# Two layers of gated cross-attention and experts: layer 0's step in another order, the experts' scores in another PSUM bank

## The chip, the cores and the metric

One core of a Trainium2 chip. The metric is the device time of one execution in microseconds; the median of three runs before is 2903.76 us (2900.48 to 2905.07). In the profile PE is TensorE's matmuls, PEld its weight loads, DVE VectorE, ACT ScalarE, POOL GpSimd and SP the engine that issues most DMAs. "L599" is line 599 of the kernel before.

## The reference

The input x is 64 sequences of 128 positions by 128 features; a context has 64 sequences of 77 positions. Two layers follow one another, each of a cross-attention and an expert block, added to x through a gate:

```python
x = x + tanh(g_xattn[0]) * L0_xattn(ctx, ctx, layernorm(x), ...)   # 16 heads, features exp(z), exp(-z)
x = x + tanh(g_ffn[0])   * L0_ffn(layernorm(x), ...)               # 8 experts, silu(g) * u, inner 336
x = x + tanh(g_xattn[1]) * L1_xattn(layernorm(x), ctx, ctx, ...)   # 16 heads, relative positions
x = x + tanh(g_ffn[1])   * L1_ffn(layernorm(x), ...)               # 8 experts, top 2, relu(h)**2
```

Layer 0's attention maps queries, keys and values of each head to 16 features, takes softmax(q k / sqrt(128)), weighs the value features and multiplies the 256 outputs by fc_w. Its expert block has a router (softmax over 8 experts) and a small "actor" network that chooses how many of the experts count for a position. Every expert is computed for every position; a position's score for an expert, or 0, multiplies that expert's output row:

```python
for e in range(E):
    g = einsum('bsh,ih->bsi', hidden, gate_w[e])
    u = einsum('bsh,ih->bsi', hidden, up_w[e])
    y = einsum('bsi,hi->bsh', silu(g) * u, down_w[e])
    out = out + scores[..., e:e + 1] * y
```

## The kernel before

**Units and groups.** Layer 0's attention works on units of two sequences (32 units), its expert block and the whole of layer 1 on groups of four sequences (16 groups). Two units make a group.

**Layer 0's step.** Step k is a software pipeline over five pieces of work, each a Python generator whose parts are cut by `yield`:

- `l0_features(k)`, five parts: loads x and context (xg, cg), layer norm, transposes into pt and copies (L295 to L299); the projection pz (L302) and four Exp; transposes pv of the value features with copies to va (L318, L320); the split of the features into three bf16 parts (`split3`, L126 to L129: two casts on DVE, two subtractions on POOL); then ten DMAs through DRAM that stack them as qst and kst (dq, dk, then L331 and L333).
- `l0_maxima(k-1)`, seven parts: six banks of scores S (L346) with a maximum each (L349); then the transposition pn (L354), whose three bf16 parts n go by three DMAs into rows 96 to 98 of qst (L362).
- `l0_weighted(k-2)`, nine parts: the scores ST again (L387), now with the maximum folded in, Exp to P (L390), and the weighted sum AV (L376); then through DRAM to the normalized o (`normalize`, L437).
- `l0_project(k-3)`, one part: the output product pf (L411) and the sum x1 (L413).
- in even steps from 4 on `route`, six parts, for the group whose second half `l0_project` has just made: layer norm; transposes ptf (L449); router and actor product pr; logits pl (L469 to L474); softmax and ranks on DVE; and `scores_out`, whose transposes pp (L590) give the scores s3 in bf16 (L593).

Beside them runs the "tape", the expert blocks: 33 parts per group in layer 0 (`l0_ffn`), 24 in layer 1 (`l1_ffn`), some 16 of them in each step of layer 0. A part is one block of hidden units (gate product pg, up product pu, three matmuls each, then tanh and multiplications to t, and its two halves hh and hl) or one expert's output: `score_in` spreads the expert's score over all partitions by a matmul with a selection matrix (pb, `spread`, L599) and a copy to sb (L604), six matmuls make the output rows py, and `add_expert` multiplies py by sb (ys, L613; L610 for the first expert) and adds to acc. Once per group of layer 0 another `spread` makes the scale sl (L548) for the leftover hidden units, whose output rows are collected in one py over five blocks. `flush` (L570 on) transposes acc into po and stores a finished group.

**The order.** `weave` runs the parts of all pieces in order of due times. A row `(lo, hi, pri)` of `PLAN` spreads a piece's parts evenly from lo to hi, in shares of the step; parts due at the same time go in the order of the list, in which `out` stands first. With `pri` above 0 the part's instructions are emitted under `high_priority(offset=pri)`. From the emitted program the tile framework makes a fixed order of instructions on each engine, sets the waits, and gives buffers out; at run time every engine's queue is worked off in that order.

**The banks.** PSUM has eight banks of 128 x 512 float32. In layer 0 they are: `pmisc` (tag misc), `pS`, `pST`, `avp`, `pY` (tag y), and three `pGU` (tag gu). The pools misc, S, ST and y have one buffer each, so that a tile there waits until the tile before it has been read. Users of misc in layer 0 are pt, pz, pv (twice), pn, pf, pl, pp and pb; users of y are py and po. The units of layer 1 use misc for pc, px, pz (three), pv, po1, po2 and pf, its routing for ptf, pr, pl and pp, and its experts for pb.

**Other buffers that matter here.** xg has four buffers, kst and va three, qst three, o two, hh, hl and t three each, sb one, x1 three.

After layer 0's 34 steps a transition joins the last unit's output product and the last routing of layer 0 to the first units of layer 1, in a step of its own that takes its numbers from `PLAN["out"]` and `PLAN["rt0"]`.

Of the kernel before, what the change touches and what calls it, by code (L numbers as in the profile page):

```python
# [10 lines left out]
F32 = mybir.dt.float32  # L11
# [30 lines left out]
def weave(tc, streams):  # L42
# [18 lines left out]
PARTS0, PARTS1 = 33, 24  # L61

PLAN = dict(
    out=(0, 0.2, 2000),
    wei=(0, 0.7, 0),
    max=(0.2, 0.95, 1000),
    fea=(0.2, 0.6, 1000),
    out1=(0.25, 0.4, 600),
    att1=(0.1, 0.95, 0),
    rel1=(0.37, 0.93, 0),  # L70
# [7 lines left out]
    prjT=(0, 0.55, 1000),  # L78
    attL=(0.1, 0.4, 500),
    prjL=(0.2, 0.3, 500),  # L80
    rt0=(0.1, 1, 500),
    rt1=(0.45, 0.7, 1000),
)

# [11 lines left out]
class Net:  # L96
# [498 lines left out]

    def spread(self, w, s3):

        pb = self.pmisc.tile([128, 512], F32, tag="misc", name="pb")
        self.nc.tensor.matmul(pb, lhsT=w, rhs=s3, start=True, stop=True)  # L599
        return pb  # L600

# [442 lines left out]
    def run(self, ngroups):  # L1044
# [25 lines left out]
        nun = ngroups * 2  # L1070
        st = {}
        for k in range(nun + 2):
# [13 lines left out]
            if k == 1:  # L1086
                with tc.issue_after(self.last_dma.ins):
# [11 lines left out]
        self.banks = itertools.cycle(((self.pS, "S"), (self.pST, "ST")))  # L1099
        s1 = {}  # L1100
        h0, h1 = (0, 0, 2), (0, 2, 2)
        self.step([(self.l0_project(nun - 1, st.pop(nun - 1), self.xs), 1, *PLAN["out"]),
                   (self.route(ngroups - 1), 6, *PLAN["rt0"]),
                   (self.l1_project(*h0, s1), 8, *PLAN["prjT"]),
                   (self.l1_relate(h0, s1), 7, *PLAN["relT"])], 27, PLAN["t0"])
        self.step([(self.l1_attend(s1[h0], 2), 13, *PLAN["attL"]),
# [140 lines left out]
```

## Time and profile before

| | us |
|---|---|
| median of three runs | 2903.76 (2900.48 to 2905.07) |
| the profiled execution | 2871.89 |
| its span, first to last instruction | 2870.2 |
| mean granted TensorE clock in it | 0.921 |
| spread matmul pb (L599), 265 records | 409 ns each, 108.3 in all |
| copy sb (L604), 256 | 587 ns each, 150.3 in all |
| multiplication ys (L613), 224 | 684 ns each, 153.2 in all |
| output product pf (L411), 256 matmuls of 128 columns | 312 ns each, 40.9 in all |
| layer 0's steps | about 0 to 1400 us; in the steady part a pair of steps takes about 87 us |
| the transition | about 1400 to 1600 us |
| layer 1 | about 1500 to 2870 us |

The profiled execution is shorter than the runs' median by 1.1%. The busy time of an engine is the time in which one of its instructions ran; a wait is idle time of an engine, put down to what released it last. Of the time in which an engine waits, only that which the end of the program depends on costs anything.

### The profile page before, as it was taken

How to read it: one execution, taken by the hardware profiler on the slowest of the kernel's cores; microseconds unless marked ns; L12 is line 12 of the kernel's file. 1: busy time of each engine (PE TensorE's matmuls, PEld its weight loads, DVE VectorE, ACT ScalarE, POOL GpSimd, SP SyncE). 2: the span in 40 equal slices, each digit the busy share in tenths (PEclk: the TensorE clock that was granted, in tenths of full speed). 3: DMA queues.
4: the chain of work that ended last, by engine and by line, in shares of the span. 5: the costliest groups of instructions: out<-in, count | busy, mean ns of one | idle time of the engine just before them, and what ended most of it. 6: DMA issues, size and time to landing. Idle time of an engine off the chain costs nothing.

```text
span 2870.2 us, 61032 instructions
## 1 busy us (share of the span) xinstructions
PE 2452.1 (85%) x23631; PEld 1668.7 (58%) x23638; DVE 1935.3 (67%) x4054; ACT 1579.2 (55%) x3030; POOL 1574.0 (55%) x1508
## 2 busy tenths in 40 slices
PE   3788898888888888988887878898988889889887
PEld 2455665666566565656554556566665666556654
DVE  3468787777878778777764555566566666656655
ACT  2455565555555555555543445566655556556556
POOL 4455555565545555455645535565555556555556
PEclk9989999999999999999986778899999999999998
DMA  6743534544445445343244655554554556555500
GB/s 144 163 103 96 106 91 83 116 98 95 97 84 105 107 93 101 87 85 77 77 84 108 137 104 119 116 110 108 109 115 104 118 119 126 116 105 113 108 16 8
DMA packets 504412, 290.56 MB, mean 101 GB/s; under 512 B 264614, under 2 KB 480814, under 8 KB 504027
## 3 DMA queue, kind: packets, MB, share of 16 engines
q1 hardware_dynamic: 476475, 246.28, 42.8%
q10 hardware_dynamic: 27648, 40.38, 4.0%
q8 instruction: 186, 3.05, 0.4%
q14 instruction: 103, 0.84, 0.1%
HBM read 147.19 MB, written 138.60 MB: 100 GB/s over the span
## 4 chain that ended last, share of the span: by engine, by line
PE 42%; DVE 19%; DMA 18%; POOL 8%; issue 7%; ACT 4%; SPq 3%; ACTq 0%; POOLq 0%; DVEq 0%
PE py L156 3%; PE ST L827 3%; PE py L157 3%; DMA qst<-dq 2%; DMA qst<-n 2%; PE py L158 2%; PE AV L376 2%; PE pz L156 2%; DVE t L508 2%; PE pg L156 2%; POOL hl L987 2%; PE S L770 2%; DVE t L509 2%; DMA kst<-dk 2%; PE ST L387 2%
## 5 line engine op out<-in xcount | busy, mean ns | idle before, releaser
L515 POOL TENSOR_TENSOR hl<-t,hh 128x512 fp32r<-128x512 f32 x336 | 454.0, 1357 | 345.3 <-ACT hh L514 339.0
L987 POOL TENSOR_TENSOR hl<-t,hh 128x512 fp32r<-128x512 f32 x256 | 345.2, 1362 | 111.6 <-ACT hh L986 111.1
L819 POOL TENSOR_TENSOR sc<-sc,mx 128x308 f32<-128x308 f32 x256 | 192.1, 752 | 216.0 <-DVE mx L818 139.5
L507 ACT ACTIVATE t<-pg 128x512 f32<-128x512 f32 x336 | 200.7, 598 | 160.6 <-PE pg L158 104.3
L514 ACT CAST hh<-t 128x512 fp32r<-128x512 f32 x336 | 207.8, 619 | 137.4 <-DVE t L509 58.0
L613 DVE TENSOR_TENSOR ys<-sb,py 128x512 f32<-128x512 f32 x224 | 153.2, 684 | 190.0 <-ACT sb L604 105.0
L828 ACT ACTIVATE rel<-ST 77x512 f32<-77x512 f32 x256 | 157.9, 617 | 187.3 <-PE ST L827 185.7
L508 DVE SCALAR_TENSOR_TENSOR t<-t,pg 128x512 f32<-128x512 f32 x336 | 226.8, 675 | 40.7 <-ACT t L507 40.2
L509 DVE TENSOR_TENSOR t<-t,pu 128x512 f32<-128x512 f32 x336 | 226.7, 675 | 10.8 <-PE pu L158 3.8
L604 ACT COPY sb<-pb 128x512 f32<-128x512 f32 x256 | 150.3, 587 | 134.7 <-PE pb L599 88.5
L817 DVE TENSOR_TENSOR sc<-S,rq 128x308 f32<-128x308 f32 x256 | 121.4, 475 | 147.8 <-PE ST L827 73.2
L986 ACT CAST hh<-t 128x512 fp32r<-128x512 f32 x256 | 158.5, 624 | 109.8 <-PE py L158 82.7
L614 POOL TENSOR_TENSOR acc<-acc,ys 128x512 f32<-128x512 f32 x96 | 133.6, 1391 | 154.5 <-DVE ys L613 154.2
L390 ACT ACTIVATE P<-ST 77x512 f32<-77x512 f32 x256 | 151.1, 591 | 120.3 <-PE ST L387 115.5
L979 ACT ACTIVATE t<-pz 128x512 f32<-128x512 f32 x256 | 153.3, 599 | 71.6 <-POOL hl L987 64.3
L827 PE MATMUL ST<-ident,sc 128*128 128x128 f32 (+1 forms) x1024 | 182.8, 307 | 5.1 <-ACT sg L776 1.6
L349 DVE TENSOR_REDUCE mx<-S 128x5 f32<-128x385 f32 (+1 forms) x192 | 110.3, 576 | 107.4 <-PE S L346 106.5
L156 PE MATMUL pu<-xh,wu_h 128*128 128x512 f32 x336 | 159.1, 473 | 21.9 <-DVE t L508 20.7
L156 PE MATMUL pg<-xh,wg_h 128*128 128x512 f32 x336 | 161.4, 480 | 15.7 <-DVE t L509 10.2
L157 PE MATMUL py<-hl,wd_h 128*128 128x512 f32 x336 | 150.9, 449 | 23.3 <-POOL hl L515 22.8
L156 PE MATMUL py<-hh,wd_h 128*128 128x512 f32 x336 | 152.0, 452 | 17.8 <-DVE ys L613 13.4
L827 PEld LDWEIGHTS ST<-ident,sc 128*128 128x128 f32 (+1 forms) x1024 | 131.7, 157 | 43.3 <-issue 14.2
(248 smaller groups left out, 6572.1 us busy)
## 6 DMA issues: line engine op xcount, KB each, us to landing
rq<-ra SPq DMA_DIRECT2D x256, 154.0 KB
qst<-dq SPq DMA_DIRECT2D x96, 384.0 KB
ra<-sg ACTq DMA_DIRECT2D x128, 192.5 KB
kst<-dk SPq DMA_DIRECT2D x96, 231.0 KB
dq<-f SPq DMA_DIRECT2D x47, 384.0 KB
od<-av SPq DMA_DIRECT2D x32, 512.0 KB
ra<-sg ACTq DMA_DIRECT2D x64, 231.0 KB
dq<-f SPq DMA_DIRECT2D x47, 256.0 KB
```

What stands on the lines that cost most here:

```text
L156: nc.tensor.matmul(ps, lhsT=wh, rhs=xh, start=start, stop=False)
L157: nc.tensor.matmul(ps, lhsT=wh, rhs=xl, start=False, stop=False)
L507: nc.scalar.activation(t, pg, AF.Tanh, scale=0.5)
L508: nc.vector.scalar_tensor_tensor(t, t, 1.0, pg, ALU.add, ALU.mult)
L509: nc.vector.tensor_tensor(t, t, pu, ALU.mult)
L514: nc.scalar.copy(hh, t)
L515: nc.gpsimd.tensor_tensor(hl, t, hh.bitcast(F32), ALU.subtract)
L819: nc.gpsimd.tensor_tensor(sc, sc, m.unsqueeze(2).to_broadcast([128, 4, KL]), ALU.subtract)
L827: nc.tensor.transpose(st[:r, j, :], sc.rearrange("q j k -> q (j k)")[:, j * KL : j * KL + r], self.ident)
L828: nc.scalar.activation(relg[:KL, hg, b], st[:KL].rearrange("k j (q e) -> k j q e", e=2), AF.Exp, scale=1.0 / math.sqrt(HD))
L986: nc.scalar.copy(hh, t)
L987: nc.gpsimd.tensor_tensor(hl, t, hh.bitcast(F32), ALU.subtract)
```

## The change

In `PLAN`, layer 0's features move from 0.2 to 0.6 of the step to 0 to 0.15, the output product from the step's start to 0.16, and routing from 0.1 to 0.2; the priorities stay. The transition keeps the old numbers under the new names `outT` and `rtT`. In `spread` the tile pb is taken from the pool `pY`, tag y, in place of `pmisc`, tag misc; since both `score_in` and the leftover's scale call it, and both layers' experts call `score_in`, every pb of the program moves. What is computed is the same.

```diff
 PLAN = dict(
-    out=(0, 0.2, 2000),
+    out=(0.16, 0.2, 2000),
+    outT=(0, 0.2, 2000),
+    rtT=(0.1, 1, 500),
     wei=(0, 0.7, 0),
     max=(0.2, 0.95, 1000),
-    fea=(0.2, 0.6, 1000),
+    fea=(0, 0.15, 1000),
...
-    rt0=(0.1, 1, 500),
+    rt0=(0.2, 1, 500),
...
     def spread(self, w, s3):
 
-        pb = self.pmisc.tile([128, 512], F32, tag="misc", name="pb")
+        pb = self.pY.tile([128, 512], F32, tag="y", name="pb")
         self.nc.tensor.matmul(pb, lhsT=w, rhs=s3, start=True, stop=True)
         return pb
...
-        self.step([(self.l0_project(nun - 1, st.pop(nun - 1), self.xs), 1, *PLAN["out"]),
-                   (self.route(ngroups - 1), 6, *PLAN["rt0"]),
+        self.step([(self.l0_project(nun - 1, st.pop(nun - 1), self.xs), 1, *PLAN["outT"]),
+                   (self.route(ngroups - 1), 6, *PLAN["rtT"]),
                    (self.l1_project(*h0, s1), 8, *PLAN["prjT"]),
                    (self.l1_relate(h0, s1), 7, *PLAN["relT"])], 27, PLAN["t0"])
```

## The prediction

> **What bounds the kernel now.** First the page: the span, the busy shares, the granted clock.
>
> ```profile
> span 2870.2 us, 61032 instructions
> PE 2452.1 (85%) x23631; PEld 1668.7 (58%) x23638; DVE 1935.3 (67%) x4054; ACT 1579.2 (55%) x3030; POOL 1574.0 (55%) x1508
> PEclk9989999999999999999986778899999999999998
> ```
>
> TensorE is the fullest engine and no other comes near it, so time can only be won from its gaps. Next the busy time by stretch (columns: length, then PE, PEld, DVE, ACT, POOL busy, granted clock, DMA share, GB/s).
>
> ```profile
> 64.00:100.00 36.00, 17.87 (x155) 11.61 (x154) 8.48 (x21) 14.98 (x33) 17.56 (x18) 1.00 0.75 185
> 200.00:400.00 200.00, 178.25 (x1211) 122.01 (x1210) 161.25 (x317) 116.08 (x228) 112.77 (x96) 0.97 0.47 102
> 2000.00:2400.00 400.00, 358.48 (x4702) 247.08 (x4704) 252.18 (x579) 237.75 (x450) 232.81 (x235) 0.93 0.54 114
> ```
>
> Layer 0's steady part keeps PE busy 89% of the time (178.25 of 200), layer 1 90%. The seven such stretches from 200 to 1400 us leave 141 us idle; that is the most that layer 0 has to give. Third, who waits for whom. The first four lines are of the whole run, the last four are PE's own waits between 150 and 1450 us (total us, times, longest).
>
> ```profile
> ACT sb L604 <- PE pb L599: 88.5, 89, 4.9
> DVE ys L613 <- ACT sb L604: 105.0, 54, 4.0
> SPq L135 <- DVE f L128: 124.8, 29, 7.7
> PE S L770 <- DMA qst<-dq: 26.4, 15, 6.6
> ...
> PE S L346 <- DMA kst<-dk: 55.0, 24, 4.8
> PE py L157 <- POOL hl L515: 21.9, 17, 4.4
> PE pu L156 <- DVE t L508: 20.7, 33, 1.5
> PE ST L387 <- ACT P L390: 3.4, 5, 0.7
> ```
>
> Last the timeline of one pair of steps, cut to the users of the bank "misc" and what stands at its door.
>
> ```profile
> 663.80 0.54 DVE L349 TENSOR_REDUCE mx<-S 128x5 f32<-128x385 f32 x1
> 667.63 0.39 PE L590 MATMUL pp<-identb,p3b 128*24 128x128 bf16 x4
> 670.84 0.38 PE L599 MATMUL pb<-s,sel 128*128 128x512 bf16 x1
> 673.50 1.05 PE L411 MATMUL pf<-fcw,o 128*128 128x128 f32 x8
> 677.01 0.39 PE L599 MATMUL pb<-s,sel 128*128 128x512 bf16 x1
> 678.64 0.38 PE L295 MATMUL pt<-ident,ln_xn 128*128 128x128 f32 x2
> ...
> 693.10 0.58 ACT L604 COPY sb<-pb 128x512 f32<-128x512 f32 x1 [0.77 <-PE pb L599]
> 696.13 0.42 PE L354 MATMUL pn<-ident,mx 128*32 128x128 f32 x1
> 700.75 1.61 PE L411 MATMUL pf<-fcw,o 128*128 128x128 f32 x8
> 704.30 0.38 PE L295 MATMUL pt<-ident,ln_xn 128*128 128x128 f32 x2
> ```
>
> Each user of misc comes exactly in the order in which the program emits it (even step: pf, pt, pz, pv, pv, pb, pl, pb, pn, pp, pb, pb; odd: pf, pb, pt, pz, pv, pv, four pb, pn), however long another has been ready. So misc is a queue. The last row of maxima was reduced at 664.34 (663.80 + 0.54), and pn, which needs only that, ran at 696.13, behind four pb: 31.8 us late. The next two units' pn were 11.5 us late (726.65 to 738.13) and 28.5 us late (757.39 to 785.85). The normalized input of the pt at 678.64 was complete at 628.1, 50 us before. The attention chain, the routing and the experts hold one another up in this one bank.
>
> **The change, part by part.** *The spread (L598) goes to the bank y.* Nine pb of each group of layer 0 and eight of layer 1 leave the misc queue: 16 x 17 = 272. Then pn no longer waits for an expert's score copy, nor an expert for routing's pp. What this frees is PE's waiting on attention's transfers and on an FFN that runs alone. In layer 0 the first kind is 55.0 for kst (L346) and 6.0 for n (L387), 61.0 us; the second is 21.9 + 20.7 and 30.6 in smaller rows (py behind ys 13.4, pg 9.5 and 4.7, hh 3.0), 73.2 us. The ends are nothing and all 134 us. I take a third of the first, 20 us: S still stands directly behind its transfer in an in-order queue, and only the half of the units with the long pn wait gains much. Of the second I take a fifth, 15 us: these hops stay, and only the stretches in which the FFN had no attention work beside it go. Layer 1 loses the same coupling; the waits there that this can reach are 25.0 (L770 for qst after 1450 us), 4.5 (pz for sb) and 3.7 (pb for sb), 33.2 us, of which I take a third, 11 us, between nothing and 33. DVE's 105.0 us behind sb end too, for sb now precedes py in the bank; I count nothing, since DVE at 67% sets no end.
>
> *Its price in y.* Until now py's first matmul could follow the multiply of the expert before at once: ys ended at 691.56, py began at 691.62. Now pb, the wait for ACT and the copy stand between: pb at 686.52, copy ended at 687.85, 1.33 us. Nothing covered, this is 272 x 1.33 = 362 us; at best it is nothing. The nearest row is ST (L387), also one bank, also matmul, a 0.59 us ACT pass, matmul: its 256 such chains cost PE 3.4 us there and 3.9 us on the weight load of AV (L376), 0.029 us each. By it, 272 x 0.029 = 8 us lost. I take that, because gate and up matmuls (three gu banks, a separate set) stand beside it as other work did beside ST. Without that cover it would be the 1.33 each. What is queued behind a py that waits on PE is everything, S and ST too.
>
> The Trainium skill's page Perfetto Trace Analysis (§ Optimizing Tensor Performance, Matmuls) speaks against this move: independent matmul groups should rotate through different PSUM banks, so that the evacuation of one overlaps the next group's matmuls. Here the evacuation of pb would overlap none of py's. The row of ST shows the price of such a shared bank as 7.3 us in 256; read strictly, the rule would put the uncovered 362 us in place of my 8.
>
> *Features to 0 to 0.15, ahead of the output product.* Two layer norms, four transposes, one projection (pz), four more transposes, four Exp, three copies, one POOL add (0.79), the split (0.63 + 1.75 + 0.85 + 1.84 us on DVE and POOL) and twelve SP transfers (xg, cg, six of dq and dk, four of qst and kst) move up in each of 32 steps. Nothing is added. On SP the twelve pass the store of x2d (L580) alone; output product and routing issue none there. On POOL the split's 3.6 us moves ahead of routing's 1.0 us power (L114) in even steps. SP's wait for the split (L135, 124.8 us in 29) can hold the three rows of n, 4.3 us each: 0 to 16 x 4.3 = 69 us; I take nothing, for n's rows then come some 20 us earlier than now. The gain in the steady part lies in the 61.0 already counted. In the fill there is one more: the fourth features' pt waits at 93 us for the first pf at 89, though pn of the step before ran at 63.8. PE idles 18.1 of the 36 us from 64 to 100; half, 9 us, between nothing and 18.
>
> *Output product behind features, routing behind both.* pf now follows four users of misc: from pt to the end of the second va copy it took 7.0 us (767.2), 7.8 (678.6), 13.2 (704.3) and 15.2 (791.4), mean 10.8. On the routing side that is 16 x 10.8 = 173 us at worst. I take nothing: the second pf of a pair stood behind a pn that was some 30 us late, and that lateness goes first. If the cover fails, the next to be late is x1, then ptf, pl, pp and the new group's first sb.
>
> *The transition* keeps its old numbers (outT, rtT): nothing.
>
> Sum: -20 - 15 - 11 + 8 - 9 = -47 us of the profiled execution's 2871.9 (span 2870.2), which is 1.1% under the runs' median of 2903.76. 47/2871.9 = 1.64%; of 2903.76 that is 48, so **2856 us**. Its own range, from a third of these gains to one and a half: 2830 to 2888.
>
> **Rivals.** *Large gain (0.08):* half of every wait listed goes, 67 in layer 0, 17 in layer 1, all 18 of the fill, less 8: -94 us, 2809. For it: how late pn is. Against: PE is at 89% already, DVE at 81% of the steady stretch (161.25 of 200), both in order.
>
> *Nothing (0.09):* attention comes earlier and then waits for PE, which was busy all along; within 0.2% of 2904, 2898 to 2910 (about the smallest change a measurement of this kernel can tell). For it: only 11% of the time is idle. That the move does not free pn, because something else in misc holds it, ends here too.
>
> *Slower, y becomes the bound (0.14):* a quarter of the 1.33 us shows: 0.25 x 362 = 90 lost against 55 gained, +35 us, 2939. It decides from 55/362 = 15% uncovered. For it: y already holds the leftover sum through five hidden blocks, and the FFN then runs on three hh buffers. Against: the ST row.
>
> *Slower, routing late (0.13):* half of the 173 us shows, 86 - 47 = +39, 2943. For it: routing's chain from pf at 700.75 to pp at 757.6 is 57 of the pair's 87 us. Against: the 30 us that pn gives back.
>
> **Numbers.** The forecast has 0.56. Faster by over 0.2%: 0.56 + 0.08 = 0.64; the same 0.09; slower 0.14 + 0.13 = 0.27. The range reaches from the large gain's 2809, rounded to 2805, up to 2925, halfway into the slower cases: about 0.05 is left out below and 0.13 above.
>
> **What would show it.** Right: pn within some 5 us of its last maximum; pt directly behind pp or pn, no longer 3.7 us behind pf; no DVE wait of ys for sb; S in the stretches where none ran (673 to 707 us); PE's wait for kst below 55 us. Price: a new PE wait of py or pb for ACT sb or DVE ys, 8 us in all. Wrong: that wait above 55 us, or pp further from the pf before it than 57 us with PE idle beside it, or the granted clock of the steady part, 0.97 in the stretch shown, falling as PE fills.

## The result, and the profile after

The changed kernel takes 2929.82 us (median of six runs, 2923.87 to 2944.74) against 2896.57 us before (2886.53 to 2905.07) on the same chips: a ratio of 1.0123, 95% interval [1.0088, 1.0158]. It is slower, and above the range that was stated.

The profiled execution before, 2871.9, lies below all six of its runs, and the one after, 2944.7, is the longest of its six, so the traces show 72.8 us of difference where the medians show 33. What follows uses the traces for where the time sits and the ratios for how much it is. The page of the changed kernel:

```profile
span 2943.0 us, 61153 instructions
PE 2464.7 (84%) x23607; PEld 1687.2 (57%) x23638; DVE 1884.6 (64%) x4054; ACT 1570.6 (53%) x3030; POOL 1561.5 (53%) x1508
PEclk9989988998998989988999788999999999999999
```

TensorE is less full than before, not fuller. The busy time by stretch (columns as before) says in which stretches:

```profile
64.00:100.00 36.00, 15.71 (x146) 10.09 (x146) 6.42 (x11) 13.97 (x30) 16.31 (x14) 1.00 1.01 214
200.00:400.00 200.00, 171.25 (x1178) 116.69 (x1179) 146.84 (x297) 106.77 (x212) 106.23 (x94) 0.94 0.41 94
2000.00:2400.00 400.00, 353.23 (x4808) 244.36 (x4802) 252.33 (x607) 239.82 (x454) 233.44 (x241) 0.94 0.58 118
```

In layer 0's steady part DVE fell from 161 to 147 us of 200: the same work goes by more slowly. In layer 1 PE does more matmuls in the same 400 us (4808 for 4702). In the fill the profile's DMA share reaches 1.01 (0.75 before). A clock for the stages is the copy of a group's scores to s3 (L593 before, L595 after), once per group, read from the timeline:

| | before | after | difference, us |
|---|---|---|---|
| first scores | 148.4 | 167.4 | +19.0 |
| first to last scores of layer 0 | 1317.2 | 1401.5 | +84.3 |
| a pair of steps in it, mean of twelve | 87.75 | 95.27 | |
| to the first scores of layer 1 | 168.3 | 162.5 | -5.8 |
| first to last scores of layer 1 | 1187.7 | 1167.9 | -19.8 |
| a group of layer 1, mean of thirteen | 80.93 | 79.44 | |
| rest of the span | 48.5 | 43.7 | -4.8 |

So the change gains 30 us from the transition on, where only the spread's bank is new, and loses 103 before, where both edits act. The waits of the whole run (total us, times, longest):

```profile
ACT sb L606 <- PE pb L601: 155.1, 105, 7.1
PE S L348 <- DMA kst<-dk: 92.1, 25, 11.1
PE ST L389 <- DMA qst<-n: 41.1, 19, 5.8
PE pb L601 <- DVE ys L615: 14.9, 32, 2.6
PE py L158 <- ACT sb L606: 11.6, 21, 0.9
```

DVE's 105 us behind sb are gone from the list, as foretold, and the price of the shared bank, py behind sb, is small. But PE waits longer for kst (92.1 for 75.3 us) and for n (41.1 for 19.4). The timeline of one pair, cut to the users of misc and to the features' input:

```profile
728.33 0.39 PE L592 MATMUL pp<-identb,p3b 128*24 128x128 bf16 x4
730.86 0.38 PE L297 MATMUL pt<-ident,ln_xn 128*128 128x128 f32 x2
737.65 1.05 PE L413 MATMUL pf<-fcw,o 128*128 128x128 f32 x8
739.57 0.48 DVE L415 SCALAR_TENSOR_TENSOR x<-pf,tgates,xg 128x256 f32<-128x256 f32 x1
741.52 0.39 SPq L289 DMA_DIRECT2D xg<-in_x_dram  x1
742.08 0.27 PE L356 MATMUL pn<-ident,mx 128*32 128x128 f32 x1
745.59 0.47 DVE L111 BATCH_NORM_STATS2 ln_st<-xg 128x6 f32<-128x128 f32 x2
748.89 1.16 POOL L116 TENSOR_TENSOR ln_rs<-ln_rs,mhalf 128x2 f32<-128x2 f32 x1
751.81 2.57 DVE L121 TENSOR_SCALAR ln_xn<-xg,ln_mv,ln_rs 128x128 f32<-128x128 f32 x2
756.21 0.39 PE L297 MATMUL pt<-ident,ln_xn 128*128 128x128 f32 x2
771.59 1.16 PE L413 MATMUL pf<-fcw,o 128*128 128x128 f32 x8
822.99 0.39 PE L592 MATMUL pp<-identb,p3b 128*24 128x128 bf16 x4
```

Here the answer stands in order. At 739.57 the output product's sum reads an xg for the last time. Only then, at 741.52, is the load of x for the next features issued: it goes into the buffer just read. The load, the layer norm on DVE and POOL and the transposition take until 756.21. In all eleven such places between 300 and 1350 us the pt comes 14.2 to 15.7 us after the load. And the next pf, which starts routing, stands in misc behind that pt and the three tiles after it.

The pair's 94.7 us are this loop: pp to pf 9.3, pf to the load 3.9, the load to pt 14.7, pt to the next pf 15.4, pf to the next pp 51.4. Before, the output product ran ahead of its step's features, so xg's oldest buffer came free one features earlier. There too each load was issued within 1 us of the sum that freed its buffer, but the pt that needs it came 25 to 65 us later, and the normalized input lay ready 17 to 54 us before its transposition (1.5 to 5.6 us before every second pt of the changed kernel).

### The profile page after: what moved, and what is told of

The parts are those of the page before. It is cut to its first block, busy times and chain, and to the rows that moved or that the text cites. A ratio compares the mean times of both kernels' runs of the same rounds, so it can differ in the third digit from the quotient of the medians.

```text
span 2943.0 us, 61153 instructions
## 1 busy us (share of the span) xinstructions
PE 2464.7 (84%) x23607; PEld 1687.2 (57%) x23638; DVE 1884.6 (64%) x4054; ACT 1570.6 (53%) x3030; POOL 1561.5 (53%) x1508
## 4 chain that ended last, share of the span: by engine, by line
PE 47%; DMA 21%; DVE 17%; issue 4%; POOL 4%; SPq 4%; ACT 2%; DVEq 0%; ACTq 0%; POOLq 0%
DMA kst<-dk 4%; PE py L158 3%; PE ST L829 3%; PE py L159 3%; DMA den<-od 3%; PE py L160 3%; DMA rp<-rd 3%; DMA dk<-f 3%; PE AV L837 2%; PE pu L158 2%; DMA od<-av 2%; PE pg L158 2%; PE S L772 2%; PE AV L378 2%; DMA rq<-ra 2%
## 5 line engine op out<-in xcount | busy, mean ns | idle before, releaser
L517 POOL TENSOR_TENSOR hl<-t,hh 128x512 fp32r<-128x512 f32 x336 | 459.8, 1374 | 564.3 <-ACT hh L516 533.9
L989 POOL TENSOR_TENSOR hl<-t,hh 128x512 fp32r<-128x512 f32 x256 | 348.2, 1373 | 213.0 <-ACT hh L988 209.5
L510 DVE SCALAR_TENSOR_TENSOR t<-t,pg 128x512 f32<-128x512 f32 x336 | 226.5, 674 | 103.3 <-ACT t L509 102.7
L615 DVE TENSOR_TENSOR ys<-sb,py 128x512 f32<-128x512 f32 x224 | 151.8, 678 | 80.9 <-PE py L160 71.5
L829 PE MATMUL ST<-ident,sc 128*128 128x128 f32 (+1 forms) x1024 | 173.8, 295 | 17.9 <-ACT rel L830 8.0
L158 PE MATMUL pg<-xh,wg_h 128*128 128x512 f32 x336 | 167.7, 499 | 12.3 <-DVE t L511 6.5
L348 PE MATMUL S<-kst,qst 96*128 96x77 bf16 x1024 | 78.8, 219 | 112.0 <-DMA kst<-dk 92.1
L829 PEld LDWEIGHTS ST<-ident,sc 128*128 128x128 f32 (+1 forms) x1024 | 125.2, 151 | 59.0 <-issue 22.6
L348 PEld LDWEIGHTS <-qst 96*128 96x128 bf16 x1024 | 61.5, 110 | 158.9 <-issue 144.9
```

The lines of the kernel that those rows point to most:

```text
L158: nc.tensor.matmul(ps, lhsT=wh, rhs=xh, start=start, stop=False)
L510: nc.vector.scalar_tensor_tensor(t, t, 1.0, pg, ALU.add, ALU.mult)
L517: nc.gpsimd.tensor_tensor(hl, t, hh.bitcast(F32), ALU.subtract)
L615: nc.vector.tensor_tensor(ys, sb, py, ALU.mult)
L829: nc.tensor.transpose(st[:r, j, :], sc.rearrange("q j k -> q (j k)")[:, j * KL : j * KL + r], self.ident)
L989: nc.gpsimd.tensor_tensor(hl, t, hh.bitcast(F32), ALU.subtract)
```

## The experiments

Theory A: the new order is the loss. Reversing output product and features makes xg's four buffers one too few, the load of x enters the loop, and the output product stands behind those features in misc. Theory B: the loss is the price of the bank y. Theory C: the early features themselves, or routing's later start. Each run is timed against the kernel before on the same chip.

| run | ratio to before | 95% interval | first scores | pair | group of layer 1 |
|---|---|---|---|---|---|
| the change | 1.0123 | 1.0088 to 1.0158 | 167.4 | 95.27 | 79.44 |
| e1 spread alone | 0.9792 | 0.9755 to 0.9829 | 148.6 | 86.33 | 79.42 |
| e2 order alone | 1.0279 | 1.0242 to 1.0315 | 167.1 | 93.24 | 81.85 |
| e3 change, five xg | 0.9752 | 0.9716 to 0.9787 | 162.0 | 85.24 | 79.64 |
| e4 before, five xg | 0.9865 | 0.9834 to 0.9896 | 149.9 | 85.04 | 81.82 |
| e5 spread, old order, five xg | 0.9785 | 0.9771 to 0.98 | 150.2 | 87.38 | 79.60 |
| e6 change, output product first | 0.9779 | 0.9763 to 0.9795 | 151.9 | 86.69 | 79.48 |
| e7 change, features back | 0.9782 | 0.9768 to 0.9797 | 148.7 | 86.59 | 79.46 |
| e8 as e6, five xg | 0.9865 | 0.984 to 0.989 | 152.5 | 88.27 | 79.66 |
| e9 spread, old order, three xg | 1.0 | 0.998 to 1.002 | 155.2 | 90.04 | 79.13 |
| e10 as e3, steps 0 to 4 in the old order | 0.977 | 0.9737 to 0.9803 | 150.1 | 84.77 | 79.64 |
| e11 change, pf in y | 1.0027 | 1.0009 to 1.0044 | 155.4 | 90.75 | 79.49 |

**The two halves of the change, each alone.** e1 is the kernel before with one line changed:

```diff
-        pb = self.pmisc.tile([128, 512], F32, tag="misc", name="pb")
+        pb = self.pY.tile([128, 512], F32, tag="y", name="pb")
```

> Only the spread scores move to the bank y; layer 0 keeps its old order. Theory A (the loss lies in the new order: the loads of x for the next features wait for the output product, and the output product stands behind those features in the bank misc): a pair of layer 0's steps takes at most the 87.5 us of before, a group of layer 1 about 79 us as in the changed kernel, ratio to before 0.975 to 0.995. Theory B (the loss is the price of the shared bank y in layer 0): the pair takes about 95 us, ratio 1.01 to 1.03.

e2 is the changed kernel with this line turned back.

> Only layer 0's order changes; the spread scores stay in misc. Theory A: a pair of steps takes at least 93 us, a group of layer 1 stays at 81 us, ratio to before 1.015 to 1.05, slower than the changed kernel, which has layer 1's gain. Theory B: the pair stays at 87.5 us or falls, ratio 0.985 to 1.005.

Measured: 0.9792 and 1.0279. The spread's move gains 2.1%, the order loses 2.8%, and the product of the two, 1.0065, is near the whole, 1.0123, within the intervals. A group of layer 1 takes 79.1 to 79.7 us wherever the spread is in y and 80.9 to 81.9 wherever it is in misc. Theory B falls. What the bank y costs PE in e1 is in its own waits:

```profile
PE pb L599 <- DVE ys L613: 14.9, 29, 2.7
PE py L156 <- ACT sb L604: 12.3, 26, 0.7
```

The first takes the place of py's wait for ys of before (19.6 us), the second is new.

e2 is slow by the expected amount, but it is not held in the same place. Its normalized input is complete at 738 us, and the transposition that needs it runs 15 us later, behind five score tiles and pn in misc:

```profile
737.12 0.60 DVE L121 TENSOR_SCALAR ln_xn<-xg,ln_mv,ln_rs 128x128 f32<-128x128 f32 x2 [1.19 <-POOL ln_rs L116]
744.81 0.27 PE L356 MATMUL pn<-ident,mx 128*32 128x128 f32 x1
753.23 0.63 PE L297 MATMUL pt<-ident,ln_xn 128*128 128x128 f32 x2
```

Every second pt of e2 comes 12.5 to 16.5 us after its input is ready. So while the score tiles are still in misc, that pt waits for its turn and not for the load of x. Theory A's second half, the queue, fits this; e2 with a fifth buffer was not run, so it is not shown.

**A buffer for x.** e3 is the changed kernel, e4 the kernel before, each with

```diff
-        xg = self.f0.tile([128, NU, 128], F32, tag="xg", bufs=4, name="xg")
+        xg = self.f0.tile([128, NU, 128], F32, tag="xg", bufs=5, name="xg")
```

> The changed kernel with five buffers of xg in place of four, so that x for the next features can be loaded before the output product has read the oldest. Theory A: the transposition pt of every second features comes about 14 us earlier, the pair takes 80 to 88 us in place of 95, ratio to before 0.96 to 0.995. Theory B (bank y) and theory C (routing alone is late, for it starts later in the step): no change, pair 94 to 96 us, ratio 1.005 to 1.02.

> The control: the kernel before with five buffers of xg. There the normalized input is complete 20 to 50 us before its transposition, so all theories expect no change: pair 87.5 us, ratio 0.995 to 1.005.

Measured: e3 0.9752, pair 85.24. One buffer of x takes 10.0 us off each pair and turns the loss into the largest gain of the study. The timeline of e3, in the same place of the loop:

```profile
756.38 0.39 PE L592 MATMUL pp<-identb,p3b 128*24 128x128 bf16 x4
759.40 0.60 DVE L121 TENSOR_SCALAR ln_xn<-xg,ln_mv,ln_rs 128x128 f32<-128x128 f32 x2 [1.96 <-PE pt L297]
766.46 1.05 PE L413 MATMUL pf<-fcw,o 128*128 128x128 f32 x8
770.37 0.64 SPq L289 DMA_DIRECT2D xg<-in_x_dram  x1
776.29 0.38 PE L297 MATMUL pt<-ident,ln_xn 128*128 128x128 f32 x2
791.50 1.33 PE L413 MATMUL pf<-fcw,o 128*128 128x128 f32 x8
```

The normalized input for the pt at 776.29 is complete at 760.00 (759.40 + 0.60), before the output product has run; the load at 770.37 is for a later one. The leg from pf to pt is 9.8 us where the changed kernel had 18.6, and the other legs hardly differ (10.1, 15.2 and, to the next pp at 841.8, 50.3).

e4 was not what all theories expected: the kernel before gains 1.35% from the same buffer. Its pt follows the output product's sum by 0.7 or 2.0 us, much as before (0.3 to 2.8 in nearly every step), so it isn't this loop. One wait does go: between 200 and 1400 us the load of x (L287) held the SP queue for 103.3 us in 13 waits before, and for 6.4 in e4. But in e1 it holds it for 246.9 us and still for 231.9 with the fifth buffer (e5, below), so the gain of e4 stays unexplained.

**Which part of the order.** e6 is the changed kernel with `out=(0, 0.2, 2000)`, e7 with `fea=(0.2, 0.6, 1000)`. Either puts the output product ahead of the features again; e6 leaves the features early, and both leave routing at 0.2.

> The changed kernel with the output product back at the step's start, so that it is emitted ahead of the features, which stay at 0 to 0.15; routing stays at 0.2; four buffers of xg. Theory A (the output product behind the features is the loss, by the slot of xg and the queue of misc): pair 84 to 88 us, first scores at about 150 us, ratio to before 0.970 to 0.985. Theory C (the features' early place itself, or routing's late start): pair stays above 92 us, ratio 1.005 or more.

> The changed kernel with only the features back at 0.2 to 0.6, so that the output product at 0.16 is again ahead of them; routing stays at 0.2; four buffers of xg. Theory A: pair 85 to 88 us, ratio 0.975 to 0.985, as with the spread alone (0.979). Theory C with routing's late start as the cause: pair above 92 us, ratio 1.005 or more.

Measured: 0.9779 and 0.9782, both as fast as the spread alone. Early features cost nothing, routing's later start costs nothing; theory C falls. Only the crossing of output product and features does the harm.

**With and without the order, all with five buffers.** e5 is e1, e8 is e6, each with the fifth buffer.

> Layer 0's old order, the spread in the bank y and five buffers of xg, without the change's order. If the new order costs nothing once x has a buffer (it only needed the slot), this equals the changed kernel with five buffers: ratio to before 0.970 to 0.980. If the order costs on its own (the fill, where the first scores came 13 us later, and the output product behind the features), this is faster: 0.958 to 0.969, pair of steps 82 to 84 us, first scores at 148 to 150 us in place of 162.

> The output product first, features right behind it, the spread in y, five buffers of xg: what each part is thought to give, together. Theory A: at least as fast as the best of the others, ratio to before 0.955 to 0.972, pair 82 to 85 us. If TensorE itself is the limit by then, no better than the changed kernel with five buffers: 0.972 to 0.978.

Measured: e5 0.9785, e8 0.9865. e5 is no faster than e1, so the buffer's gain in e4 and the spread's do not add. e8 misses its expectation: the parts that each gained something are together slower by 0.9% than e6 alone, with a pair of 88.27 us. Why isn't known. The fixed order of every engine is made anew for each variant, which may be the reason; no run shows it. So a difference of some 2 us per pair between two variants says little about the idea behind them. The 10.0 us of e3 are far above that, the 1.4 us by which e1's pair is shorter than before are not.

**The wait put back, in the old order.** e9 is e1 with three buffers of xg.

> The wait put back without the new order: layer 0's old order and the spread in y, as in the run with the spread alone (0.979, pair 86.3 us), but three buffers of xg, so that x for the next features is loaded only after the output product just ahead of them has read its own. Theory A (the slot of xg sets the pair): every pt comes 10 to 16 us after the output product's sum in place of 1 to 4, pair 91 to 100 us, ratio to before 1.00 to 1.04. Theory D (the new order is slow for another reason, for example the output product behind four users of misc): pair 85 to 88 us, ratio 0.975 to 0.985.

Measured: 1.000 [0.998, 1.002] against e1's 0.9792; pair 90.04 against 86.33. The pt now comes 9 to 14 us after the output product's sum in nearly every step (0.6 to 4 in e1). The late buffer alone, with the order untouched, costs 3.7 us a pair: theory A's direction, with ratio and pair at or just below the low end of what it expected. The crossing costs 8.6 us a pair (95.27 against e6's 86.69). The loop puts the other 5 to the output product that waits behind the late pt; no run shows that part by itself.

**The queue of misc.** e11 takes the changed kernel's pf from y.

```diff
-        pf = pm.tile([128, 512], F32, tag="misc", name="pf")
+        pf = self.pY.tile([128, 512], F32, tag="y", name="pf")
```

> The changed kernel, four buffers of xg, with the output product's bank pf taken from y in place of misc: it is still emitted behind the features but no longer stands behind them in the queue of misc. Theory A with the queue as a necessary part of the loop: the sum of the output product comes earlier than the features of its step, x is loaded earlier, pair 84 to 88 us, ratio 0.97 to 0.985. If the slot alone decides and the queue of misc does not: pair stays at 93 us or more, ratio 1.005 or more.

Measured: 1.0027, pair 90.75, between the two expectations. The output product leaves the queue of misc, but in y it stands behind the experts (one pf ran 23 us after its step's second pv). Every second pt still comes 17 to 19 us after the load of x, but its normalized input is ready 9.7 to 11.1 us before it, so the load is no longer what that pt waits for. The load itself waits longer, at the head of the SP queue for the sum: 181.1 us in 23 waits between 200 and 1400 us, 70.8 in 12 in the changed kernel. So this run doesn't separate the two links; it moves the output product to another queue, and what sets its 90.75 us was not found.

**The fill.** e10 is e3 with the old order in steps 0 to 4.

> The changed kernel with five buffers of xg, and the old order in steps 0 to 4 alone. Theory A: the first scores come at 148 to 153 us in place of 162, the pair stays at 84 to 87 us, ratio to before 0.968 to 0.975. If the fill's loss is only moved, the later steps give it back and the ratio stays at 0.975 to 0.98.

Measured: first scores at 150.1 in place of 162.0, pair 84.77, but 0.977: the two spans are equal, 2822.9. In e10's trace the fill is 12 us and the steps of layer 0 are 6 us shorter than in e3's, but the transition is longer (171.5 us for 160.1), and so are layer 1 and the end (2 and 4 us). So the time won back in the fill did not reach the end of the program.

## Why the prediction was wrong

The forecast was 2856, faster; the kernel is slower, 2929.82.

**The step that failed is "output product behind features", priced at nothing.** The prediction priced the four users of misc in front of pf, 10.8 us a step, and let the late pn pay for them. What it did not ask is which buffer the moved step must wait for. xg has four buffers; features(k) loads into the one that l0_project(k-4) reads. In the old order that read stood at the start of the step before, with one features between it and the features that wait for it; in the new one no features stand between them. The term is the 14.7 us from the load to pt and what stands behind it in misc. With the fifth buffer, and the score tiles out of misc, the step does cost about nothing (e3, pair 85.24 against e1's 86.33), so there the assumption was right but for the slot. With the score tiles in misc it was not even that: e2 loses 2.8% although x lies ready 12.5 us or more before its pt. Of the rivals, "y becomes the bound" came nearest in number, 35 us slower against 33 measured, by luck: e1 has the same bank y and is faster. "Routing late", 2943, looked at the path from pf to pp, but that leg got shorter, 51.4 for 56.9 us; the legs ahead of it grew.

**The spread's move: right in kind, and its sizes were off.** The sum gave it -38 us (20, 15 and 11 gained, 8 lost). Alone it gained 2.1%, about 60 us. The price in y, "py or pb for ACT sb or DVE ys, 8 us in all", is 27.2 us in e1 (12.3 and 14.9); less the 19.6 us of py behind ys that it replaces, that is 7.6, as the row of ST had it. The gain stood elsewhere than foretold: 11 us were counted in layer 1, and a group there takes 1.5 us less, which in e1's trace is 22 us over layer 1 with 6 more in the transition and 5 in the tail; of the 35 of layer 0 that trace shows 10. The claim that pn would run within 5 us of its last maximum is wrong: before it was late by 13 and 30 us on average in the two kinds of step, in e1 by 10 and 19, in the changed kernel by 26 in both. The score tiles were only a part of what stood ahead of it; the output product's and the features' turns in misc remain. Nor does the lateness of pn set the pair: in e3, the fastest, it is 9.5 and 28.5. A slip without effect on the sum: the stretches of 200 us from 200 to 1400 us are six and not seven; their 141 us of idle time are right.

The Trainium skill's page Perfetto Trace Analysis (§ Optimizing Tensor Performance, Matmuls) asks that independent matmul groups rotate through banks. e1 goes against the rule and is 2.1% faster: with all eight banks taken, moving pb out of one shared bank into another cost 7.6 us more of waiting there and took the score tiles out of the queue of attention and routing.

**The fill: the sign was wrong.** The fourth features did come earlier, at 65.8 instead of 93.1 us, as foretold. But their transfers then stood beside the experts' weight loads and those that make o: the DMA share of 64 to 100 us rose from 0.75 to 1.01. The last transfer ahead of the first o was issued 11.3 us later, first before, then after:

```profile
83.86 0.33 SPq L436 DMA_DIRECT2D rr<-dr  x1
```

```profile
95.16 2.65 SPq L438 DMA_DIRECT2D rr<-dr  x1
```

The runs agree: in the changed kernel, e2, e3 and e11 the fourth features' pt runs at 66 to 67 us, the share is 0.98 to 1.01 and this transfer is issued at 95 to 97; in all others pt runs at 93 to 99, the share is 0.75 to 0.80 and the transfer goes at 84 to 89. The prediction moved PE's idle time and did not price the twelve transfers against those already in flight. The first scores came 19.0 us later where 9 had been counted as gained; with the old order in the first steps (e10) they are back at 150. That transfer is only a part of the 19 us: e11 has it as late and its first scores at 155.4.

**The granted clock fell** in layer 0's steady part, which the prediction had named as a sign against itself. It expected that to come with a fuller PE; it came with an emptier one, as the last section shows.

## What to carry to other kernels

When a step is moved past another, ask of every buffer it fills who reads that buffer last, and where that reader now stands; a count of buffers that was enough in one order is one short in the other, and the trace shows it as a load issued right behind the read of the same buffer, with its consumer right behind the load. The first half alone says nothing: in both orders the loads stood right behind the reads, and only the time from load to consumer told them apart, 25 to 65 us against 14 to 16 in every second step. A bank with one buffer is a queue in program order: moving a frequent, independent tile out of a queue that ties several chains together can pay even where the new bank is shared. Take a change of two parts apart before judging it: here one part gained 2.1% and the other lost 2.8%.

## What the runs showed of the hardware

TensorE's gaps cost more than their length. One gap of the changed kernel: S waits 4.94 us for kst up to 791.42. The stretches around it (PE busy first, granted clock third from the right):

```profile
784.00:787.00 3.00, 2.48 (x11) 1.34 (x9) 1.28 (x2) 2.90 (x7) 1.66 (x2) 1.00 1.20 184
787.00:790.00 3.00, 0.00 (x0) 0.00 (x0) 0.00 (x0) 0.44 (x1) 1.19 (x1) 0.85 1.26 191
790.00:793.00 3.00, 0.69 (x7) 0.53 (x7) 1.68 (x3) 0.00 (x0) 0.00 (x0) 0.50 0.38 88
793.00:796.00 3.00, 3.00 (x11) 2.04 (x11) 2.15 (x4) 0.00 (x0) 0.00 (x0) 0.51 0.49 87
```

The clock was at 1.00 before the gap and at 0.50 after it, also while PE was wholly busy again (793 to 796). In the clock record of each trace there are only these two values, and between 200 and 1400 us of the traces before, after and of e3 each spell at 0.50 lasts 3.4, 6.8, 10.2 or 13.7 us. In these stretches there are 40 gaps of 2.5 us or more between matmuls; 39 of them are followed by the start of such a spell within 5 us of their end or have it inside. Per pair of steps the spells sum to 8.2 us before, 16.8 in the changed kernel and 5.7 in e3. So PE's busy time per pair rose from 77.4 us (1058.76 of 1200, pair 87.75) to 81.4 (1025.63 of 1200, pair 95.27) with the same matmuls: some 4 of the 7.5 us that a pair lost are a slower clock, the rest idle time. This holds for these two executions. The profiled one of the changed kernel has the lowest clock of its six over the whole run (0.921; the others 0.923 to 0.930), and the one before has 0.921 too: the fall is in layer 0 alone, where the mean from 200 to 1400 us is 0.91 for 0.95. The Trainium skill's page TensorE: Matmul & The Clock Gate (§ HAM oscillation — how this bites in real kernels) describes this: a wait for data long enough for the activity monitor lets the clock fall back to half, and the work behind it starts cold. The trace agrees, at 0.50 and in steps of 3.4 us. But no single wait has to be that long: for 59 of the 77 spells in the three traces, no gap in the 6.9 us ahead of the spell was over 3.4 us, the length that the section names.
